# A four-layer graph network on one core: edges on 125 partitions, self-counts in the count matrix, norm sums on VectorE

## The chip, the core and the metric

The kernel runs on one core of a Trainium2 chip. The core has five engines, each with its own in-order queue: PE (TensorE, matrix products; its weight loads are listed as PEld), DVE (VectorE), ACT (ScalarE), POOL (GpSimd) and SP (SyncE, which here only issues DMAs). DMAs are issued from SP, ACT and POOL and are carried by the core's 16 DMA engines. The metric is device time in microseconds (us) of one execution; lower is better.

## What is computed

A graph of N = 6250 nodes with D = 64 features and E = 206250 edges, sorted by destination, goes through four layers, and after each of them `x = layernorm(x + layer(x))`:

```
layer 0: Z[n] = sum over edges e into n of relu([x[src[e]], edge_attr[e]] @ M_W.T + M_b);  relu([x, Z] @ U_W.T + U_b)
layer 1: two GCN convolutions, 64 -> 32 -> 64, relu between
layer 2: attention with 4 heads over the edges into each node (softmax by destination), + bias + x
layer 3: two GCN convolutions, 64 -> 64 -> 64, batch norm over the nodes and leaky relu after each
gcn(h, W, b)[n] = sum over e into n of h'[src[e]] * d[src[e]] * d[n]  +  h'[n] * d[n]^2  +  b,
                  h' = h @ W,  d = rsqrt(in-degree + 1)
```

The second term of `gcn` is each node's own contribution (its self-loop).

## The kernel before

**Tiling.** Nodes stand in NB = 49 blocks of L = 128, the last with NL = 106. Edges stand in supertiles of L partitions with J = 30 successive edges each: LJ = 3840 edges, so S = 54 supertiles, of which the last has only LP = 91 partitions (`of(s)` gives the number). The order of all instructions is the order of the program text (`manual_schedule`); each engine's queue is in that order.

**Start (lines 96 to 424, 707 to 748).** SP loads `x`, then all destinations `dst_i` (L126, L128, L129: rows of 30 integers, 120 bytes each), some weights, then three copies of the edge list on 125 partitions with 1650 edges each (`ef` L350, `en` L352, `sf` L354), two tiles of edge features `xe` (L643), the sources `src_i` (L126, L128, L129 again), `hl_d`, and some thirty small weights and rows. ACT writes the table `tab_d` of transformed nodes to DRAM. VectorE makes from the destinations the window positions `dst_w` and the digits `dst_h`, `dst_l`; from `ef`, `en`, `sf` a check and `hl`; from the last weights (L730 to L739) some products; from `src_i` the row numbers `src_sb` (L133 to L135); and adds up `x_part` (L745). Only then does it come to the loop of layer 0.

**Layer 0 (lines 749 to 782).** Iteration s issues the fetches of supertile s (SP: `xe`, 960 KB; POOL: 30 indirect gathers of one row of `tab_d` per partition into `g`, L433, three buffers) and computes supertile s - 1 (`messages`): PE turns `xe` (L662) and multiplies it (L676), VectorE adds to `g` (L680) and copies `we` (L682), ACT takes relu (L687), VectorE makes one-hot rows of the destinations (L474), and 60 PE instructions (L484) add the messages up in a window, which VectorE adds to `acc` (L487). At five places in each supertile `fill()` puts in one step of a side job. The first side job, `degrees`, is S steps of counting (VectorE: L524, L527; PE: L518) and one that closes it; it gets the first n_count = S // 5 + 1 = 11 iterations. The second, `adjacency`, takes the other S - n_count = 43: 25 count matrices of 2 x 128 destinations by all sources, in 8 steps each (VectorE: one-hots L591, L594 and a check L610; PE: L603; ACT: L605 to fp8), which ACT sends to `adj_d` (L613, 1568 KB each). Side operands such as `iota_c` stand in PSUM. The last supertile goes through `last_messages`.

**Layers 1 and 3** are each two calls of `aggregate`: 13 groups of up to four node blocks. In a group PE multiplies the features (split into three bf16 parts) with the count matrices that SP loads back from `adj_d` (L862, L871); ACT takes the sums out (L843); PE adds the node's own features through the identity (L846) and folds the parts (L848); then comes `post`. In layer 3 `post` is that of `sums_for`: it scales and shifts, and adds up h and h^2 over all nodes for the batch norm with two PE products by a matrix of ones per group (L1194, L1195) into two PSUM banks.

**Layer 2 (lines 1015 to 1094)** gathers 54 x 30 rows of `tab2_d` by `src_sb` (POOL), writes them out by edge (`rows_d`), reads them back as runs by node, and works on these.

The loops of `general`, `general_attention` and `message_sums`, at the end, run only when a check finds data that the fast path can't take; they don't run with these inputs.

Of the kernel before, what the change touches and what calls it, by code (L numbers as in the profile page):

```python
# [39 lines left out]
LF = 125  # L41
# [14 lines left out]
def tile_gnn_resnorm(ctx: ExitStack, tc, a, out, J):  # L56
# [7 lines left out]
    LJ = L * J  # L64
    S = -(-E // LJ)
    LP = (E - (S - 1) * LJ) // J
    EP = E // LF
# [5 lines left out]
    assert E == LF * EP and E == (S - 1) * LJ + LP * J and L <= 2 * LP and EP <= J * L // 2  # L73
# [48 lines left out]

    def load_edges(o, v, s0, s1=S):

        full = min(s1, S - 1)
        nc.sync.dma_start(o[:, s0:full, :], v[s0 * LJ:full * LJ].rearrange("(s p j) -> p s j", p=L, j=J))  # L126
        if s1 == S:
            nc.sync.dma_start(o[0:LP, S - 1, :], v[(S - 1) * LJ:E].rearrange("(p j) -> p j", j=J))  # L128
            nc.sync.dma_start(o[LP:L, S - 1, :], v[E - (L - LP) * J:E].rearrange("(p j) -> p j", j=J))  # L129

# [24 lines left out]
    dst_w = keep.tile([L, S, J], F32, name="dst_w")  # L155
    src_sb = keep.tile([L, S, J], I32, name="src_sb")
# [115 lines left out]
    src_1 = pk.tile([L, S1, J], I32, name="src_1")  # L272
    dst_h = pk.tile([L, S, J], BF16, name="dst_h")
    dst_l = pk.tile([L, S, J], BF16, name="dst_l")
    ohd = st0.enter_context(tc.tile_pool(name="ohd", bufs=2))
# [5 lines left out]
    src_i = pp.tile([L, S, J], I32, name="src_i")  # L281
    lo_i = pp.tile([L, S, J], I32, name="lo_i")
    dig_f = pp.tile([L, EP], F32, name="dig")
    dig = dig_f[:, 0:S * J].rearrange("p (s j) -> p s j", j=J)

    def early(pool, shape, name, like, dtype):

        t = pool.tile(like, dtype, name=name)
        n = 1
        for k in shape[1:]:  # L290
            n *= k
        f = "p j w -> p (j w)"
        return (t.rearrange(f)[0:shape[0], 0:n * 4 // (2 if dtype == BF16 else 4)]).bitcast(I32)

    dst_i = early(ohd, [L, S, J], "oA", [L, J, L], BF16).rearrange("p (s j) -> p s j", j=J)
    d_f = dst.rearrange("(p i) -> p i", p=LF)
    ef = early(ohp, [LF, EP], "oh", [L, J // 2, W], F32)
    en = early(ohp, [LF, EP], "oh", [L, J // 2, W], F32)
    sf = early(ohd, [LF, EP], "oA", [L, J, L], BF16)
    nc.scalar.dma_start(src_i[:, 0:S1], src[0:S1 * LJ].rearrange("(s p j) -> p s j", p=L, j=J))  # L300
    load_edges(dst_i, dst, 0)
# [34 lines left out]
    def ends_in(b):  # L336

        return min(S, -(-(a_block * (b + 1) + SLACK + R) // LJ)) - 1
# [14 lines left out]
    nc.sync.dma_start(en[0:LF - 1, EP - 1:EP], d_f[1:LF, 0:1])  # L353
    nc.sync.dma_start(sf, src.rearrange("(p i) -> p i", p=LF))  # L354
# [3 lines left out]
    in_psum = ps_c.tile([128, W + 1 + 2 * NB], F32, name="pc")  # L358
# [6 lines left out]
    for i in range(2):  # L365
        nc.vector.tensor_copy(iota_2[i * R:(i + 1) * R, i * NB:(i + 1) * NB], iota[i * R:(i + 1) * R, 0:NB])

# [25 lines left out]
    ends = small.tile([L, 2, S], F32, name="ends")  # L393
# [3 lines left out]
    for i, op in enumerate((OP.min, OP.max)):  # L397
        pe = ps_t.tile([S, L], F32, name="pt")
        nc.tensor.transpose(pe, ends[:, i, :], ident[:L, :L])
        nc.vector.tensor_reduce(end2[:, i:i + 1], pe, AX.X, op)  # L400
# [11 lines left out]
    pb = ps_t.tile([L, S], F32, name="pt")  # L412
    nc.tensor.matmul(pb, ones[0:1, :L], win_f[:, 0, :], start=True, stop=True)
    base_b = small.tile([L, S], F32, name="base_b")
    nc.vector.tensor_copy(base_b, pb)
    nc.vector.tensor_sub(dst_w, dst_w, base_b[:, :, None].to_broadcast([L, S, J]))

    d_e = dig_f[0:LF]
    nc.vector.tensor_sub(d_e, ef, en)
    nc.vector.tensor_reduce(bad4[0:LF, 0:1], d_e, AX.X, OP.max)  # L420
    nc.vector.tensor_copy(d_e, sf)
    hl = pp.tile([LF, EP, 2], BF16, name="hl")
    digits(hl[:, :, 0], hl[:, :, 1], sf, en, d_e)
    nc.vector.tensor_scalar_add(hl[:, :, 0], hl[:, :, 0], 1.0)

    def of(s):

        return LP if isinstance(s, int) and s == S - 1 else L

# [13 lines left out]
    def at(t, s):  # L443

        return t[0:of(s), s] if isinstance(s, int) else t[:, ds(s, 1)].rearrange("p o j -> p (o j)")

    def edges_of(t_d, s):

        n = of(s) * J
        v = t_d[s * LJ:s * LJ + n, :] if isinstance(s, int) else t_d[ds(s * LJ, n), :]  # L450
        return v.rearrange("(p j) c -> p j c", j=J)

    def all_supertiles(body):

        with tc.For_i(0, S - 1, 1) as s:
            body(s)
        body(S - 1)

    def row_of_edges(pool, v, s):

        n = of(s)
        n_i = pool.tile([L, J], I32, name="n_i")
        nc.sync.dma_start(n_i[0:n], edges_of(v.rearrange("(e o) -> e o", o=1), s).rearrange("p j o -> p (j o)"))
        lo_i = pool.tile([L, J], I32, name="lo_i")
        n_f = pool.tile([L, J], F32, name="n_f")
        row_of(n_i[0:n], n_i[0:n], lo_i[0:n], n_f[0:n])
        return n_i[0:n]
# [3 lines left out]
    def one_hot(ohp, rel, j0, places):  # L471
        n = rel.shape[0]
        oh = ohp.tile([L, JH, W], F32, name="oh")
        nc.vector.tensor_tensor(oh[0:n], places[0:n, None, :].to_broadcast([n, JH, W]),  # L474
                                rel[:, j0:j0 + JH, None].to_broadcast([n, JH, W]), op=OP.is_equal)
        return oh

    def add_window(ohp, vals, c, rel, base, places=iota):
        n = rel.shape[0]
        pa = sums_in[-1].tile([c, W], F32, name="pa")  # L480
        for j0 in range(0, J, JH):
            oh = one_hot(ohp, rel, j0, places)
            for j in range(JH):
                nc.tensor.matmul(pa, vals[0:n, j0 + j, 0:c], oh[0:n, j, :], start=(j0 + j == 0),  # L484
                                 stop=(j0 + j == J - 1))
        span = acc[0:c, ds(base, W)]
        nc.vector.tensor_add(span, span, pa)  # L487
# [7 lines left out]
    def windows(s, v, window):  # L495

        rel = small.tile([L, J], F32, name="rel")[0:of(s)]
# [13 lines left out]
    def degrees(ohd, todo):  # L511
# [3 lines left out]
        def products(i, o_h, o_l):  # L515
            n = of(todo[i])
            for j in range(J):
                nc.tensor.matmul(count, o_h[0:n, j, :], o_l[0:n, j, :], start=(i + j == 0),  # L518
# [3 lines left out]
        for i, s in enumerate(todo):  # L522
            o_h = ohd.tile([L, J, L], BF16, name="oA")
            nc.vector.tensor_tensor(o_h, iota_c[:L, None, 0:L].to_broadcast([L, J, L]),  # L524
                                    dst_h[:, s, :, None].to_broadcast([L, J, L]), op=OP.is_equal)
            o_l = ohd.tile([L, J, NB], BF16, name="oB")
            nc.vector.tensor_tensor(o_l, iota_c[:L, None, 0:NB].to_broadcast([L, J, NB]),  # L527
                                    dst_l[:, s, :, None].to_broadcast([L, J, NB]), op=OP.is_equal)
# [37 lines left out]
    def adjacency(adp, ohd):  # L566
# [41 lines left out]
        def check(c, q0, adj):  # L608
# [3 lines left out]
            if q0 + QS == L:  # L612
                nc.scalar.dma_start(adj_d[c].bitcast(I8), adj.rearrange("p l a q -> p (l a q)").bitcast(I8))  # L613
# [26 lines left out]
    with st0:  # L640
        def fetch_xe(s):
            xe = l0.tile([L, J, D], F32, name="xe")
            nc.sync.dma_start(xe[0:of(s)], edges_of(xe_in, s))  # L643
            return xe

        def fetch_g(s):
            g = gp.tile([L, J, D], F32, name="g")
            gather(g, D, tab_d, at(src_1 if s < S1 else src_sb, s))
# [5 lines left out]
        def messages(pool, s, xe, g, first_time, fill=lambda: None, then=None):  # L654

            m = of(s)
            we = pool.tile([L, J, H], F32, name="we")

            def turned(k):
                pt = ps_t.tile([128, 3, L], F32, name="pt")  # L660
                for i in range(3):
                    nc.tensor.transpose(  # L662
                        pt[:, i, 0:m], xe[0:m, 6 * k + 2 * i:6 * k + 2 * i + 2, :].rearrange("p a c -> p (a c)"),
                        ident[:m, :m])
                xT = pool.tile([128, 3, L], F32, name="xT", bufs=3)
                nc.scalar.copy(xT[:, :, 0:m], pt[:, :, 0:m])  # L666
                return xT[:, :, 0:m]

            xTs = [turned(0)]
            for k in range(J // 6):  # L670
# [3 lines left out]
                pm = ps_m.tile([L, 3, 2 * CW], F32, name="pm")  # L674
                for i in range(3):
                    nc.tensor.matmul(pm[0:m, i, :], xT[:, i, :], w_bd_f, start=True, stop=True)  # L676
                fill()
                pv = pm[0:m].rearrange("p i (a c) -> p (i a) c", a=2)
                js = slice(6 * k, 6 * k + 6)
                nc.vector.tensor_add(g[0:m, js, :], g[0:m, js, :], pv[:, :, 0:D])  # L680
                if first_time:
                    nc.vector.tensor_copy(we[0:m, js, :], pv[:, :, D:CW])  # L682
                if then:
                    nc.scalar.activation(g[0:m, js, :], g[0:m, js, :], AF.Relu)
                    then(js)
            if not then:
                nc.scalar.activation(g[0:m], g[0:m], AF.Relu)  # L687
            if first_time:
                nc.sync.dma_start(edges_of(we_d, s), we[0:m])
            return g  # L690

        def last_messages(s, xe, g):

            rel, n = at(dst_w, s), of(s)
# [3 lines left out]
            def add(js):  # L698
                for j in range(js.start, js.stop):
                    nc.tensor.matmul(pa, g[0:n, j, :], ohs[j // JH][0:n, j % JH, :], start=(j == 0), stop=(j == J - 1))  # L700
# [8 lines left out]
        load_edges(src_i, src, S1)  # L709
        nc.sync.dma_start(hl_d[0:E, :].rearrange("(p i) k -> p i k", p=LF), hl)  # L710
# [40 lines left out]
        with ExitStack() as st1:  # L751
            adp = st1.enter_context(tc.tile_pool(name="adp", bufs=2))
# [602 lines left out]
```

## Time and profile before

| | |
|---|---|
| device time, median of 3 runs | 5386.54 us (5385.71 to 5386.94) |
| profiled execution, its own time | 7038.8 us |
| its span | 7036.9 us |
| busy share of the span | PE 31%, DVE 40%, ACT 11%, POOL 47% |
| mean granted PE clock | 0.625 of full speed |
| first layer-0 gather | at 22.9 us |
| first step of the loop's side job on VectorE (L524) | at 152.6 us |
| layer 0 ends (L705), layer 1 begins | at 3818 us |
| first gather of layer 2 | at 4131 us |
| last gather of layer 2 | at 6434 us |

The profiled execution took 1652 us more than the runs without a profile. A profile's row of waits names the engine that waited, its instruction and what released it; "issue" and "remote" are releases that it can't name. In a timeline row the first two numbers are start and duration, and the bracket holds the idle time of the engine just before, with its releaser.

### The profile page before, as it was taken

The page shows a single profiled execution, that of the slowest core. Times are in us where ns is not written, and L with a number is a line of the kernel's source. Part 1 is how long each engine was busy: PE and PEld are TensorE (multiplying, and loading weights), DVE is VectorE, ACT ScalarE, POOL GpSimd, SP SyncE. Part 2 cuts the span into 40 slices and gives each one's busy share as a digit, 9 for nine tenths or more (in the row PEclk, how much of TensorE's full clock was granted, in tenths as well). Part 3 has the DMA queues.
Part 4 walks back from the last instruction along what each step waited for, and adds up shares of the span by engine and source line. Part 5 has one row for each costly group of instructions (what it writes and reads, how often), then busy time and mean ns, then how long its engine had stood idle before and what let it go on. Part 6 is the DMA issues. An engine that isn't in the chain of part 4 may idle for free.

```text
span 7036.9 us, 47855 instructions
## 1 busy us (share of the span) xinstructions
PE 2174.8 (31%) x18313; PEld 1664.4 (24%) x18314; DVE 2823.7 (40%) x2744; ACT 795.3 (11%) x1615; POOL 3317.3 (47%) x3350
## 2 busy tenths in 40 slices
PE   1443333333333323333336940000000000001998
PEld 1332323232323323232335520000000000001554
DVE  3554545454544545454455213233232332332012
ACT  0000011111111211111122100000000000000011
POOL 5334353444434343444431037777777777774000
PEclk5665566666666666666666975555555555555998
DMA  3011111111111111111112733233333332333442
GB/s 79 24 31 27 31 39 40 47 42 45 43 47 42 49 39 50 37 51 37 52 40 84 287 108 102 88 100 103 91 107 93 100 100 88 100 100 115 186 156 93
DMA packets 200187, 543.55 MB, mean 77 GB/s; under 512 B 110070, under 2 KB 112386, under 8 KB 178316
## 3 DMA queue, kind: packets, MB, share of 16 engines
q0 software_dynamic: 112336, 219.94, 11.9%
q1 hardware_dynamic: 67188, 273.57, 10.5%
q10 hardware_dynamic: 20424, 46.89, 1.8%
q8 instruction: 146, 2.39, 0.1%
q14 instruction: 93, 0.76, 0.0%
HBM read 434.86 MB, written 105.30 MB: 77 GB/s over the span
## 4 chain that ended last, share of the span: by engine, by line
PE 21%; POOL 19%; another core or an unknown queue 18%; issue 16%; DVE 8%; ACT 4%; DMA 2%; DVEq 0%; ACTq 0%; POOLq 0%; SPq 0%
POOL g L433 18%; PE pA L871 8%; PE pa L484 6%; DVE oB L594 2%; ACT adj L605 2%; DVE oA L591 2%; PE pA L603 1%; PE pm L676 1%; DVE most_a L610 1%; DMA rows<-rows_d,first 1%; ACT g L687 1%; PE pt L662 1%; DVE g L680 1%; PE pm L848 1%
## 5 line engine op out<-in xcount | busy, mean ns | idle before, releaser
L433 POOL DMA_INDIRECT g<-tab_d,src_sb x3120 | 3085.1, 989 | 2936.2 <-issue 2499.8
L603 PE MATMUL pA<-oB,oA 128*128 128x98 bf16 x3200 | 301.6, 240 | 1465.1 <-ACT adj L605 956.7
L591 DVE TENSOR_TENSOR oA<-pc,hlT 128x2048 bf16<-128x2048 f32 x200 | 456.7, 2283 | 598.7 <-remote 302.9
L177 PE MATMUL pt<-ident,acc 128*128 128x128 f32 (+1 forms) x50 | 14.0, 373 | 2155.4 <-issue 1359.3
L603 PEld LDWEIGHTS <-oA 128*128 128x128 bf16 x3200 | 237.3, 117 | 1529.9 <-issue 1500.5
L484 PE MATMUL pa<-oh,g 128*64 128x128 f32 x3180 | 477.0, 326 | 363.9 <-ACT g L687 355.2
L484 PEld LDWEIGHTS pa<-oh,g 128*64 128x64 f32 x3180 | 465.7, 171 | 371.8 <-ACT g L687 371.8
L605 ACT CAST adj<-pA 128x392 fp8e4<-128x392 f32 x800 | 360.1, 488 | 1555.7 <-remote 1178.1
L177 PEld LDWEIGHTS pt<-ident,acc 128*128 128x128 f32 (+1 forms) x50 | 6.2, 173 | 2164.2 <-issue 2150.4
L871 PE MATMUL pA<-adj,three 128*32 128x512 fp8e4 (+3 forms) x4949 | 478.1, 368 | 1.8 <-ACT three L243 1.8
L1025 DVE TENSOR_TENSOR g<-g,we 128x120 f32<-128x120 f32 (+1 forms) x54 | 15.4, 285 | 1051.7 <-DMA g<-tab_d,src_sb 928.1
L676 PE MATMUL pm<-w_bd,xT 128*128 128x136 f32 (+1 forms) x1620 | 343.6, 362 | 56.1 <-issue 39.9
L594 DVE TENSOR_TENSOR oB<-pc,hlT 128x1568 bf16<-128x1568 f32 x200 | 355.7, 1779 | 0.0
L610 DVE TENSOR_REDUCE most_a<-adj 128x1 f32<-128x1568 int8 x200 | 354.8, 1774 | 0.0
L1055 DVE TENSOR_REDUCE hb<-rows 128x64 f32<-128x4096 f32 x46 | 336.6, 7318 | 0.0
L524 DVE TENSOR_TENSOR oA<-pc,dst_h 128x3840 bf16<-128x3840 f32 x54 | 224.2, 4153 | 271.3 <-remote 271.3
L680 DVE TENSOR_TENSOR g<-g,pm 128x384 f32<-128x384 f32 (+1 forms) x270 | 147.3, 545 | 446.2 <-remote 389.3
L676 PEld LDWEIGHTS pm<-w_bd,xT 128*128 128x128 f32 (+1 forms) x1620 | 298.7, 259 | 79.9 <-issue 50.0
L871 PEld LDWEIGHTS <-three 128*32 128x32 bf16 (+1 forms) x5096 | 215.0, 97 | 233.9 <-issue 19.9
L666 ACT COPY xT<-pt 128x384 f32<-128x384 f32 (+1 forms) x270 | 124.0, 479 | 1165.6 <-PE pt L662 601.3
L1043 ACT COPY same<-pA 128x256 f32<-128x256 f32 x49 | 18.3, 372 | 1992.6 <-issue 1851.5
L1052 DVE TENSOR_TENSOR rows<-rows,pA 128x4096 f32<-128x4096 f32 x49 | 216.7, 4422 | 38.5 <-issue 32.2
(253 smaller groups left out, 2579.3 us busy)
## 6 DMA issues: line engine op xcount, KB each, us to landing
adj<-adj_d SPq DMA_DIRECT2D x95, 1568.0 KB
rows_d<-g SPq DMA_DIRECT2D x53, 1020.0 KB
xe<-in_edge_attr_dram SPq DMA_DIRECT2D x53, 960.0 KB
g<-tab_d,src_sb POOLq DMA_INDIRECT x3120
adj_d<-adj ACTq DMA_DIRECT2D x25, 1568.0 KB
we_d<-we SPq DMA_DIRECT2D x53, 60.0 KB
we<-we_d ACTq DMA_DIRECT2D x53, 60.0 KB
g<-tab_d,src POOLq DMA_INDIRECT x120
```

The lines of the kernel that those rows point to most:

```text
L433: nc.gpsimd.indirect_dma_start(out=g[0:n, j, 0:c], out_offset=None, in_=table[:, :], in_offset=bass.IndirectOffsetOnAxis(ap=idx[:, j:j + 1 ...
L484: nc.tensor.matmul(pa, vals[0:n, j0 + j, 0:c], oh[0:n, j, :], start=(j0 + j == 0), stop=(j0 + j == J - 1))
L524: nc.vector.tensor_tensor(o_h, iota_c[:L, None, 0:L].to_broadcast([L, J, L]), dst_h[:, s, :, None].to_broadcast([L, J, L]), op=OP.is_equal)
L591: nc.vector.tensor_tensor(o_h, iota_c[:, None, 1:L + 1].to_broadcast([128, QS, L]), hlT[:, 0, q0:q0 + QS, None].to_broadcast([128, QS, L]) ...
L594: nc.vector.tensor_tensor(o_l, iota_2[:, None, :].to_broadcast([128, QS, 2 * NB]), hlT[:, 1, q0:q0 + QS, None].to_broadcast([128, QS, 2 * ...
L603: nc.tensor.matmul(pA[:, q].rearrange("p a l -> p (a l)"), o_h[:, q1 + q, :], o_l[:, q1 + q, :], start=True, stop=True)
L605: nc.scalar.copy(adj[:, :, :, q0 + q1:q0 + q1 + 4], pA.rearrange("p q a l -> p l a q"), saturate=False)
L610: nc.vector.tensor_reduce(most_a[:, (c * L + q0) // QS:(c * L + q0) // QS + 1], adj[:, :, :, q0:q0 + QS].bitcast(I8), AX.XYZ, OP.max)
L676: nc.tensor.matmul(pm[0:m, i, :], xT[:, i, :], w_bd_f, start=True, stop=True)
L680: nc.vector.tensor_add(g[0:m, js, :], g[0:m, js, :], pv[:, :, 0:D])
L871: nc.tensor.matmul(pa[ps, 0:nk, 0:w], t[:, b, :], adj[:, 0:nk, b, 0:w], start=start, stop=stop)
L1055: nc.vector.tensor_reduce(hb[:, b, :], rows[:, :, 0:D].rearrange("p r c -> p c r"), AX.X, OP.add)
```

## The change

Edges are now tiled on LE = 125 partitions in layer 0, in its counting and in the loops at the end. 125 x 30 = 3750 edges divide E exactly: S = 55 full supertiles. The 125 partitions hold for the tiles and for the DMAs that fill them (`dst_i`, `src_i`, `xe`, `we_d`) and for the rows of each gather; n_count becomes 55 // 5 + 1 = 12, and 43 iterations remain for `adjacency`. Layer 2 keeps 128 partitions (S2 = 54): its row numbers `src2` are made anew from the sources in layer 1 (`sources`, three DMAs and L133 to L135 once more), while `src_sb` lives only in layer 0. The pool `ohd` is opened after `prep` is closed, and the early integer tiles have places of their own instead of places inside `ohd` and `ohp`.

After a count matrix's last check VectorE adds the identity (kept in PSUM beside `iota_c`) to the 128 x 128 part that holds the block's own nodes, two per matrix, 49 in all; the matrix is then sent to `adj_d` from SP instead of ACT. L846 goes. In layer 3 VectorE adds h and h^2 into `both`, two additions per group, and one PE product with the ones follows after the last group.

```diff
-    LJ = L * J
-    S = -(-E // LJ)
-    LP = (E - (S - 1) * LJ) // J
-    EP = E // LF
+    LJ = LE * J
+    S = E // LJ
+    LJ2 = L * J
+    S2 = -(-E // LJ2)
+    LP2 = (E - (S2 - 1) * LJ2) // J
+    EP = E // LE
...
-    load_edges(dst_i, dst, 0)
+    nc.sync.dma_start(dst_i, dst.rearrange(by_edge, p=LE, j=J))
...
-    in_psum = ps_c.tile([128, W + 1 + 2 * NB], F32, name="pc")
+    in_psum = ps_c.tile([128, W + 1 + 2 * NB + L], F32, name="pc")
...
+    ident_c = in_psum[:, W + 1 + 2 * NB:]
+    nc.vector.tensor_copy(ident_c, ident)
...
             if q0 + QS == L:
-                nc.scalar.dma_start(adj_d[c].bitcast(I8), adj.rearrange("p l a q -> p (l a q)").bitcast(I8))
+
+                for a in range(min(2, NB - 2 * c)):
+                    v = adj[:, 2 * c + a, a, :]
+                    nc.vector.tensor_tensor(v, v, ident_c, op=OP.add, saturate=False)
+                nc.sync.dma_start(adj_d[c].bitcast(I8), adj.rearrange("p l a q -> p (l a q)").bitcast(I8))
...
-            xe = l0.tile([L, J, D], F32, name="xe")
-            nc.sync.dma_start(xe[0:of(s)], edges_of(xe_in, s))
+            xe = l0.tile([LE, J, D], F32, name="xe")
+            nc.sync.dma_start(xe, edges_of(xe_in, s))
...
-        load_edges(src_i, src, S1)
+        nc.sync.dma_start(src_i[:, S1:S], src[S1 * LJ:E].rearrange(by_edge, p=LE, j=J))
...
+            ohd = st1.enter_context(tc.tile_pool(name="ohd", bufs=2))
             counting = degrees(ohd, list(range(S)))
...
-            nc.tensor.matmul(pm[:, 0:nb, :], ident, v[:, bs, :], start=True, stop=False)
             for r in range(nb):
-                nc.tensor.matmul(pm[:, r, :], sa[:, r * L:(r + 1) * L], stack[0:m, 0:c], start=False, stop=(r == nb - 1))
+                nc.tensor.matmul(pm[:, r, :], sa[:, r * L:(r + 1) * L], stack[0:m, 0:c], start=True, stop=True)
...
+    def sources(k):
+
+        if k != 4:
+            return
+        n = S2 * J
+        n2, lo2, f2 = (acc[:, i * n:(i + 1) * n].rearrange("p (s j) -> p s j", j=J) for i in range(3))
+        n2, lo2 = n2.bitcast(I32), lo2.bitcast(I32)
+        nc.sync.dma_start(n2[:, 0:S2 - 1, :], src[0:(S2 - 1) * LJ2].rearrange("(s p j) -> p s j", p=L, j=J))
+        nc.sync.dma_start(n2[0:LP2, S2 - 1, :], src[(S2 - 1) * LJ2:E].rearrange("(p j) -> p j", j=J))
+        nc.sync.dma_start(n2[LP2:L, S2 - 1, :], src[E - (L - LP2) * J:E].rearrange("(p j) -> p j", j=J))
+        row_of(src2, n2, lo2, f2)
+        nc.vector.tensor_add(x, x, bc(g1_b2, D))
...
+            if first_one:
+                nc.scalar.activation(both[:, 1], h, AF.Square)
+                nc.vector.tensor_copy(both[:, 0], h)
+                return
             sq = ag.tile([L, 4, D], F32, name="sq")[:, 0:nb, :]
             nc.scalar.activation(sq, h, AF.Square)
+            n = NL if bs.stop == NB else L
+            nc.vector.tensor_add(both[0:n, 0, 0:nb, :], both[0:n, 0, 0:nb, :], h[0:n])
             yield
-            lhsT = ones_l if bs.stop == NB else ones
-            stop = bs.stop == NB
-            nc.tensor.matmul(ps_1[:, 0:nb, :], lhsT, h, start=first_one, stop=stop)
-            nc.tensor.matmul(ps_2[:, 0:nb, :], lhsT, sq, start=first_one, stop=stop)
-            yield
+            nc.vector.tensor_add(both[0:n, 1, 0:nb, :], both[0:n, 1, 0:nb, :], sq[0:n])
             if bs.stop == NB:
-                for i, p in enumerate((ps_1, ps_2)):
-                    nc.vector.tensor_reduce(stat[:, i, :], p.rearrange("p b c -> p c b"), AX.X, OP.add)
+                nc.vector.tensor_reduce(stat, both.rearrange("p i b c -> p i c b"), AX.X, OP.add)
+                pm = ps_m.tile([L, 2, D], F32, name="pm")
+                nc.tensor.matmul(pm, ones, stat, start=True, stop=True)
+                nc.vector.tensor_scalar_mul(stat, pm, 1.0 / N)
...
```

## Prediction

> **What bounds the kernel now.** I first read the busy time by stretch, cut where the stages change. Columns: stretch, its length, then busy us (and instructions) of PE, weight loads, VectorE, ACT, POOL, then granted PE clock, DMA share, GB/s.
>
> ```profile
> 153.00:3818.00 3665.00, 1307.64 (x10544) 1167.25 (x10544) 1848.96 (x1518) 579.87 (x1130) 1495.04 (x1580) 0.63 0.13 40
> 3818.00:4130.00 312.00, 298.68 (x4372) 169.00 (x4371) 95.03 (x265) 61.70 (x185) 0.00 (x0) 0.95 0.61 239
> 4130.00:6437.00 2307.00, 20.73 (x66) 13.41 (x66) 727.28 (x646) 74.51 (x148) 1719.40 (x1667) 0.50 0.31 94
> 6437.00:7037.00 600.00, 519.26 (x3176) 289.54 (x3176) 111.30 (x231) 70.38 (x136) 2.86 (x3) 0.91 0.39 150
> ```
>
> Layer 1 (second row) and layer 3 (fourth) are PE's; layer 2 (third) is POOL's gathers; in layer 0 no engine is much over half busy. So the waits come next, for 153 to 3818 us:
>
> ```profile
> POOL g L433 <- issue: 2038.9, 1506, 80.3
> PEld L603 <- issue: 1500.5, 411, 27.7
> ...
> DVE g L680 <- remote: 389.3, 31, 17.5
> DVE acc L487 <- PE pa L484: 374.4, 53, 7.8
> ```
>
> Most of layer 0's waits have no releaser on record, in pieces up to 28 us. The one that the program explains is VectorE's for the 60 products of each window: 374 us. VectorE's busy 1849, these 374 and the 153 us before make 2376 us, not 3818: 1442 us of unexplained holds, where the runs without a profile are 1652 us shorter. Layer 2's gathers start 1.25 us apart where nothing holds them (0.95 + 0.30), so its 1669 would take 2086 us, not 2307: another 221. I therefore take it that the profile itself slows these two stages. Then 2376 + 312 + 2086 + 600 = 5374, against the median of 5386.5. So in the timed runs **VectorE's queue with its wait for L484 paces layer 0**: 39 us a supertile in the second side job (from 1000 to 3600 us, 38 supertiles: busy 34.0 each, less 2 us in which successive instructions overlap, plus 7.1 of that wait). POOL has 31.1 gathers x 1.25 = 38.9 there: nearly a tie.
>
> **What starts the loop.** Timeline of the start; the last row is the 91st gather, the first that needs a used buffer:
>
> ```profile
> 38.04 25.10 SPq L128 DMA_DIRECT2D src_i<-in_src_dram  x1
> ...
> 45.02 1.88 DVE L419 TENSOR_TENSOR dig<-oh 125x1650 f32<-125x1650 int32 x1 [12.12 <-DMA oh<-in_dst_dram]
> ...
> 85.98 0.23 DVE L730 TENSOR_TENSOR wa<-wn,r_L_gnn_attn_key 128x64 f32<-128x64 f32 x1 [24.12 <-DMA r_L_gnn_attn_key<-in_L_gnn_attn_key_dram]
> ...
> 223.81 0.95 POOL L433 DMA_INDIRECT g<-tab_d,src  x1 [80.26 <-issue]
> ```
>
> VectorE waits for a small row that SP issued behind everything else; SP itself stood 25 us in the issue of `src_i`. Counting begins after that, and POOL stands until the first messages are done. A later start thus moves all of layer 0, whichever engine paces it.
>
> **The change, part by part.**
>
> *Start: +50 us.* The trace has 125-partition loads already: `ef` and `en` (1.61 MB, issued from 23.3) land at 45.0, `sf` 10 us later: 80 GB/s. DMA share while they load:
>
> ```profile
> 24.00:28.00 4.00, 0.41 (x1) 0.12 (x1) 4.00 (x4) 0.00 (x0) 3.39 (x3) 0.50 0.30 74
> 36.00:56.00 20.00, 0.26 (x3) 0.02 (x1) 4.75 (x4) 0.59 (x1) 15.42 (x16) 0.63 1.09 196
> 56.00:72.00 16.00, 0.00 (x0) 0.00 (x0) 5.82 (x11) 0.00 (x0) 12.65 (x12) 0.50 0.46 110
> ```
>
> Share 0.30, gathers included, while only 125-partition loads run; it goes over 1 once the 128-partition `xe` and `src_i` come, and falls to 0.46 for a tail. The Trainium skill ("DMA: Bandwidth & Descriptors", section on why a DMA increments its semaphore by 16) says that a DMA is split over the largest number up to 16 that divides the slowest dimensions of both sides, and from SP always over the lowest-numbered engines. That is 16 for 128 partitions and 5 for 125: 5/16 = 0.31 fits the row, and the tail fits five engines that have `ef`, `en`, `sf` to finish first. By this rule the change moves `dst_i`, `src_i` and both first `xe` onto the same five engines, ahead of what VectorE waits for. Per engine: `dst_i` 6875/5 = 1375 rows of 120 bytes instead of 424, `src_i` 1275 instead of 392: 1834 more. A row costs at most 27 ns (`dst_i`: 11.7 us from issue to use, 424 rows, beside the table's writes); I take 20: 37 us. `xe`: 2 x (188 - 60) KB at 161 KB per 10 us: 16 us. Together 53, and I take **50**, since SP's issue of the small rows, not the rings, ends last now. By the byte count alone (2% fewer partitions) it would be 0. Bounds: 0, if the small rows don't queue behind these; 66, at 27 ns. Later `xe` loads take some 12 us, under a supertile's 39, and `ohd` over `prep`'s space waits for the `hl_d` write, which SP issues ahead of the small rows.
>
> *One more supertile: +20 us.* VectorE: one counting step (L524 + L527, 5.7 from start to start), five times L680 + L682 (0.64 apart), two L474 (4.2), L487 (0.28), the wait of 7.1: 20.4. The closing step of the counting takes the new twelfth iteration nearly alone, so no other VectorE work comes with it. POOL's 30 more gathers (37.5 us) lie beside it: from the 91st gather POOL needs 51 x 37.5 + 50 x 1.25 = 1975 us and some 40 for the work behind its last gather, VectorE ten counting supertiles of 42 (seen between two L487, without the hold) and 43 of 39, so 2097: some 80 us of slack. If POOL paces, 37.5 takes the place of 20 and of the next item. Gathers with 91 partitions stand in the trace at 0.95 + 0.30, like those with 128, so 125 save nothing.
>
> *49 additions of the identity: +13 us* at 0.275 (L578, 128x128 with a PSUM operand), in VectorE's pacing queue; 0 if it has slack. SP now waits for them before it issues `adj_d`; behind that stand `we_d`, which waits for the same supertile's VectorE anyway, and the next `xe`, used a supertile later. ACT loses 25 issues of 0.33 us, beside VectorE: 0.
>
> *Layer 1: -5.5, layer 3: -30 us.* Weight loads in a layer-3 group:
>
> ```profile
> 6545.23 0.41 PEld L846 LDWEIGHTS pm<-tab,ident 128*128 128x128 f32 x2
> 6545.66 1.08 PEld L848 LDWEIGHTS pm<-stack,sa 128*128 128x128 f32 x8
> ...
> 6549.09 0.41 PEld L1194 LDWEIGHTS pa<-hb,ones 128*128 128x128 f32 x2
> 6549.52 0.41 PEld L1195 LDWEIGHTS pa<-sq,ones 128*128 128x128 f32 x2
> 6549.95 0.96 PEld L871 LDWEIGHTS <-three 128*128 128x128 bf16 x5
> ```
>
> From start to start L846 costs PE 0.43 and the two sums 0.86, with L871 queued behind. 1.29 x 24 full groups = 31, and 0.5 for the short ones. Layer 1's L846 (half the width) costs 0.22 from start to start: 24 times and two short ones, 5.5. Against it stands the end of each norm: VectorE's two additions, a longer reduction and a PE product in a row instead of two reductions, about 0.65, twice. -35.7 in all; no wait of PE for `adj` is on record, though layer 1 loads 3.1 MB per 9.3 us and might give a few us back. The busy times (14.4 + 14.5 + 14.4 and 10.7) would say -54, but they overlap. VectorE's 48 additions of 0.42 us fill idle time (111 busy of 600).
>
> *`sources`:* its loads go to SP after the first three `adj` loads, whose first buffer is free only when group 0 is done; the next `adj` isn't held. L133 to L135 (3.7 us of VectorE) lie under 9.3 us of PE per group. 0, at worst 4, and 10 if the loads collide. Layer 2 is unchanged.
>
> **Sum:** 50 + 20.4 + 13 - 35.7 = +48. The profiled execution's own 7039 would move by nearer 100, as there a supertile takes 68 us; I apply +48 to the median: **5434**.
>
> **Rivals.**
> - *No shift at the start* (12%): the wait for the row is only SP's issue, and the loads overlap. 20 + 13 - 36 = -2: 5384. For it: hardly 10 us between the rings' tail and the row. Against it: SP's 25 us in one issue.
> - *ACT's queue, faster* (8%): sending `adj_d` holds ACT, which makes the relu that the window's products wait for. Two rows of waits, 5.2 and 4.7 us, name that DMA. At 5 us for each of 25: -125, so 5309; it decides from (48 + 11)/25 = 2.4 us each. Against it: 0.33 us per issue, and the other waits there name PE or VectorE.
> - *Gathers of 125 rows are slower* (5%): spread over fewer engines, 1.4 instead of 1.25 us apiece, 1650 x 0.15 = 248, less POOL's 80 of slack: about 5600. Against it: the 91-row gathers.
> - *POOL paces* (15%): 50 + 37.5 - 36: 5438, the forecast's own side.
>
> **Numbers.** The forecast, with a start shift of 30 to 66, has 60%; 0.2% (11 us) is what a measurement can tell from no change. Slower: the forecast, POOL's case, the slow gathers: 0.78. Same: most of the first rival, 0.12. Faster: the ACT case and a start without shift with hidden additions (-15): 0.10. Range 5383 to 5467: from the unshifted start to 66 us of shift with POOL pacing and a smaller PE gain.
>
> **What would show it.** VectorE's wait before L730 ending near 135 us; DMA share about 0.3 for most of the first 120 us; 55 supertiles, unchanged gather spacing; layer-3 groups 17.05 us apart instead of 18.33. It is wrong if L730 starts before 100 us, or if ACT's waits beside `adj_d` vanish with a shorter layer 0.

## The result and the profile after

The changed kernel takes **5633.88 us** (5632.94 to 5634.22) against 5386.12 (5384.82 to 5386.94): ratio 1.046, 95% interval 1.0442 to 1.0478. The forecast was 5434 (5383 to 5467). On three of the chips used further down the kernel before itself takes 6978 to 7037 us in all of its runs, and the profile that the forecast read is as long (7038.8); the comparison here and every number not marked otherwise is from where it takes about 5386.

A second profile of the kernel before, taken where it takes 5388, stands beside that of the changed kernel (times of the same events; VectorE lines by their number in the kernel before):

| event | before, us | after, us |
|---|---|---|
| first gather of layer 0 | 22.2 | 34.2 |
| first small row used (L730) | 85.4 | 107.6 |
| first window closed (first L487) | 170.3 | 193.2 |
| layer 0 ends (L705) | 2348.8 | 2624.2 |
| first gather of layer 2 | 2657.3 | 2932.1 |
| last gather of layer 2 | 4789.1 | 5064.3 |
| span | 5386.4 | 5632.5 |

Layer 0 ends 275 us later; all behind it is 29 us shorter. Between the first closed window and the end of layer 0 lie 252 of the 275 us, so the place is the loop, not the start. One stretch inside it, first before, then after (columns as in the forecast's first view: PE, weight loads, VectorE, ACT, POOL, clock, DMA share, GB/s):

```profile
1000.00:2000.00 1000.00, 563.49 (x4447) 498.40 (x4446) 821.94 (x700) 297.65 (x608) 713.71 (x757) 0.71 0.26 73
```

```profile
1000.00:2000.00 1000.00, 505.05 (x3938) 446.81 (x3938) 745.34 (x653) 261.05 (x535) 797.47 (x665) 0.68 0.23 66
```

Every engine does less, except POOL: its 665 fetches need more time than 757 did, 1.20 us each instead of 0.94. With the 0.30 us between two of them, 665 x 1.50 fills the 1000 us: POOL never stops. The groups of the changed kernel name it; the first row is layer 2 and the start, the second the rest of layer 0 (busy us, mean ns):

```profile
L415 POOL DMA_INDIRECT g<-tab_d,src x1740 | 1684.0, 968 | 937.5 <-issue 521.1
L415 POOL DMA_INDIRECT g<-tab_d,src_sb x1530 | 1849.8, 1209 | 466.4 <-issue 450.6
```

The same line, table and bytes per row, but the second group fetches 125 rows a time and costs 1209 ns, while layer 2's 128 rows take 0.94 us. VectorE's longest waits in layer 0 (first before, from 200 to 2310 us, then after, from 200 to 2600; the last supertile is left out of both):

```profile
DVE acc L487 <- PE pa L484: 356.7, 51, 7.8
DVE hlT L586 <- PE pt L583: 11.6, 25, 0.5
```

```profile
DVE acc L466 <- PE pa L463: 370.5, 53, 7.8
DVE g L661 <- DMA g<-tab_d,src_sb: 144.8, 40, 8.7
DVE used L558 <- DMA slots<-hl_d,first: 46.0, 1, 46.0
```

Its wait for the products is as before; new are 191 us of waits for data that POOL gathers (second and third row), and no such row stood there before. In the chain that ended last, POOL has 49% of the changed kernel's span (35% before).

### The profile page after: what moved, and what is told of

It is laid out like the page before. It is cut to its first block, busy times and chain, and to the rows that moved or that the text cites. A ratio compares the mean times of both kernels' runs of the same rounds, so it can differ in the third digit from the quotient of the medians.

```text
span 5632.5 us, 48009 instructions
## 1 busy us (share of the span) xinstructions
PE 2091.8 (37%) x18244; PEld 1595.5 (28%) x18245; DVE 2865.9 (51%) x2859; ACT 783.5 (14%) x1621; POOL 3634.3 (65%) x3380
## 4 chain that ended last, share of the span: by engine, by line
POOL 49%; issue 16%; PE 15%; DMA 14%; DVE 4%; ACT 1%; SPq 0%; DVEq 0%; POOLq 0%; ACTq 0%
POOL g L415 48%; PE pA L851 10%; DMA rows<-rows_d,first 9%; DMA g<-tab_d,src 3%; DMA g<-tab_d,src_sb 2%; PE pa L463 1%; PE pm L828 1%; PE pm L183 1%; DVE oB L572 1%; POOL slots L421 1%; DVE oA L569 1%; PE pm L1053 0%; DVE oA L502 0%; DVE most_a L588 0%; DVE g L661 0%
## 5 line engine op out<-in xcount | busy, mean ns | idle before, releaser
L415 POOL DMA_INDIRECT g<-tab_d,src x1740 | 1684.0, 968 | 937.5 <-issue 521.1
L415 POOL DMA_INDIRECT g<-tab_d,src_sb x1530 | 1849.8, 1209 | 466.4 <-issue 450.6
L463 PE MATMUL pa<-oh,g 125*64 125x128 f32 x3240 | 481.5, 324 | 553.3 <-ACT g L668 544.5
L463 PEld LDWEIGHTS pa<-oh,g 125*64 125x64 f32 x3240 | 470.1, 170 | 563.3 <-ACT g L668 563.3
L657 PE MATMUL pm<-w_bd,xT 128*125 128x136 f32 x1650 | 330.1, 350 | 45.9 <-DVE we L663 26.1
L657 PEld LDWEIGHTS pm<-w_bd,xT 128*125 128x125 f32 x1650 | 279.2, 242 | 78.6 <-DVE we L663 43.3
L661 DVE TENSOR_TENSOR g<-g,pm 125x384 f32<-125x384 f32 x275 | 148.8, 541 | 190.4 <-DMA g<-tab_d,src_sb 167.5
L1034 DVE TENSOR_TENSOR pA<-rows,pa 128x256 f32<-128x256 f32 x49 | 21.0, 429 | 417.7 <-DMA rows<-rows_d,first 417.7
## 6 DMA issues: line engine op xcount, KB each, us to landing
xe<-in_edge_attr_dram SPq DMA_DIRECT2D x55, 937.5 KB
```

The source lines that it names most:

```text
L415: nc.gpsimd.indirect_dma_start(out=g[0:n, j, 0:c], out_offset=None, in_=table[:, :], in_offset=bass.IndirectOffsetOnAxis(ap=idx[:, j:j + 1 ...
L463: nc.tensor.matmul(pa, vals[:, j0 + j, 0:c], oh[:, j, :], start=(j0 + j == 0), stop=(j0 + j == J - 1))
L657: nc.tensor.matmul(pm[:, i, :], xT[:, i, :], w_bd_f, start=True, stop=True)
L661: nc.vector.tensor_add(g[:, js, :], g[:, js, :], pv[:, :, 0:D])
```

## The experiments

**1. What a gather costs by its rows, measured alone.** A kernel with nothing but 30 gathers of 256-byte rows at each of thirteen row counts, then loads of `edge_attr` on different numbers of partitions; the computation is left out.

> This kernel leaves out the whole computation. It issues 30 indirect gathers of 256-byte rows at each of 128, 127, 126, 125, 124, 120, 112, 104, 100, 96, 91, 64 and 32 rows, and then plain loads of different numbers of partitions. Theory 1 (a gather's time on POOL hangs on how its row count divides, not on its size): 125 rows take about 1.21 us as in the changed kernel, 128, 112, 96 and 64 rows about 0.94, 127 at least 1.21; in plain loads 125 partitions of xe take about 16/5 of the time of 128. Theory 2 (the rows are innocent, the gathers of the changed kernel are slowed by what runs beside them): 125 rows take 0.94 us here, like 128. Theory 3 (time goes with the number of rows): 64 rows take half of 128, and 125 a little less than 128.

Groups of this kernel (30 gathers each; the mean ns is the second number behind the bar; `g_bch` is 127 rows, `g_bce` 124, `g_bcf` 125, `g_baa` 100, `g_bcg` 126, `g_bci` 128, `g_jg` 96):

```profile
L33 POOL DMA_INDIRECT g_bch<-in_x_dram,idx x30 | 76.2, 2541 | 9.2 <-issue 9.2
L33 POOL DMA_INDIRECT g_bce<-in_x_dram,idx x30 | 38.5, 1282 | 9.1 <-issue 9.1
L33 POOL DMA_INDIRECT g_bcf<-in_x_dram,idx x30 | 35.7, 1191 | 9.1 <-issue 9.1
L33 POOL DMA_INDIRECT g_baa<-in_x_dram,idx x30 | 29.7, 991 | 9.1 <-issue 9.1
...
L33 POOL DMA_INDIRECT g_bcg<-in_x_dram,idx x30 | 29.4, 978 | 9.1 <-issue 9.1
...
L33 POOL DMA_INDIRECT g_jg<-in_x_dram,idx x30 | 27.4, 912 | 9.1 <-issue 9.1
```

128 rows took 944 ns (median). 127 rows cost 2.7 times as much as 126; 64 rows took 901, so it isn't the number of rows, and 125 was dear with nothing beside it, so theories 2 and 3 fall. Divide the rows by the largest divisor up to 16, the rule that the forecast took from the Trainium skill ("DMA: Bandwidth & Descriptors", section on why a DMA increments its semaphore by 16; it states it for DMAs issued from GpSimd too, with an exception for some direct copies): 127 over 1, 124 over 4 (31 rows), 125 over 5 (25), 100 over 10, 126 over 14 (9), 128 over 16 (8), 96 over 16 (6). From 31 to 127 rows on the busiest engine the cost grows by 1259 ns, 13.1 ns a row; 0.87 us + 13 ns per such row gives all thirteen counts to within 37 ns. The trace doesn't number the DMA engines, so their count is the rule's; measured is that the cost follows it. The 91-row gathers that I had read in the forecast are 13 x 7, so they say nothing of 125.

The loads show it as well. VectorE's copy behind each (127, 126, 125, then 124 partitions, 7680 bytes each):

```profile
595.86 0.15 DVE L41 COPY w<-w 127x1 f32<-127x1 f32 x1 [39.62 <-DMA w<-in_edge_attr_dram]
601.23 0.15 DVE L41 COPY w<-w 126x1 f32<-126x1 f32 x1 [5.21 <-DMA w<-in_edge_attr_dram]
610.91 0.15 DVE L41 COPY w<-w 125x1 f32<-125x1 f32 x1 [9.54 <-DMA w<-in_edge_attr_dram]
626.03 0.15 DVE L41 COPY w<-w 124x1 f32<-124x1 f32 x1 [14.97 <-DMA w<-in_edge_attr_dram]
```

39.6, 5.2, 9.5 and 15.0 us. 125 against 126 is 1.8 times, not the 16/5 (to 128) that I had expected. Loads of `dst` follow, in rows of 120 bytes like those of `dst_i`, on 127 and 126 partitions:

```profile
720.52 0.15 DVE L46 CAST w<-t_bch 127x1 f32<-127x1 int32 x1 [60.70 <-DMA t_bch<-in_dst_dram]
728.28 0.15 DVE L46 CAST w<-t_bcg 126x1 f32<-126x1 int32 x1 [7.60 <-DMA t_bcg<-in_dst_dram]
```

By the same rule the busiest engine has 49 x 127 = 6223 rows in the first and 49 x 126 / 14 = 441 in the second: 9.2 ns a row, where the forecast took 20.

**2. The kernel before once more**, for a profile where it takes 5388 us.

> The kernel before, once more, for a profile that the profiler does not lengthen. Expected: a span near 5385 us, layer 0 over at about 2342 (5386 less the 3008 that the changed kernel needs behind layer 0 and the 36 that layers 1 and 3 saved), gathers 1.25 us apart (0.95 + 0.30). If VectorE paced layer 0, POOL's gathers wait for buffers for some 250 us in all (1620 x 1.25 = 2025 of issue, 50 row loads at 1.25); if POOL paced it, they run without a gap, and layer 0 is over near 2150.

The span was 5386.4 and layer 0 over at 2348.8. POOL's gathers stood still for less than I had put: 1580 of them between 170.9 and 2278.1, at 1.25, leave 132 us. So VectorE's queue paces layer 0, with POOL close behind, at 41.3 us a supertile (170.3 to 2316.7 us, 52 windows).

**3. Gathers of 128 rows in the changed kernel.**

```diff
-    src_sb = pk.tile([LE, S, J], I32, name="src_sb")
-    src_1 = pk.tile([LE, S1, J], I32, name="src_1")
+    src_sb = pk.tile([L, S, J], I32, name="src_sb")
+    src_1 = pk.tile([L, S1, J], I32, name="src_1")
+    nc.vector.memset(src_1[96:L], 0)
+    nc.vector.memset(src_sb[96:L], 0)
...
-            g = gp.tile([LE, J, D], F32, name="g")
+            g = gp.tile([L, J, D], F32, name="g")
...
-            return g
+            return g[0:LE]
```

> The changed kernel, but layer 0's 1650 gathers take 128 rows (rows 125 to 127 fetch row 0 of the table and are not read). Theory 1 (125-row gathers at 1.51 instead of 1.25 us apiece pace layer 0): 1650 x 0.26 = 429 us of POOL work go, VectorE paces layer 0 again, and the time falls to 5386 + 12 to 22 (start) + 20 (one more supertile) - 34 (layers 1 and 3) + 0 to 13 (identity additions), 5384 to 5407. Theory 2 (loads from few DMA engines slow the gathers, whatever their rows): it stays near 5600. Theory 4 (the norm sums and counts hold VectorE): above 5450.

5427.35 us (1.0073 of before, 1.0056 to 1.009), some 20 over the range. **Three rows more per gather, fetched for nothing, take 207 of the 248 us away.** The gathers are at 0.94 us again, and of VectorE's waits for gathered data one of 14.0 us is left. The rest is 39 us: first window at 189.6 (+19.3), from there to the end of layer 0 53.7 more, everything behind it 34.3 less.

**4. The two other parts of the change alone**, on 128 partitions: with both parts; with only the norm sums; with only the self-counts. (The kernel has 54 supertiles, not the 49 that the first expectation names.)

> The kernel before with the two other parts of the change alone: self-counts in the count matrix, and norm sums on VectorE; edges stay on 128 partitions, layer 0 has 49 supertiles and gathers of 128 rows. Theory 1: layers 1 and 3 save their 34 to 36 us, the identity additions cost 0 to 13, so 5350 to 5365, faster than before. Theory 4 (these parts cost time themselves): 5390 or more.

> The kernel before with one part of the change: layer 3's norm sums on VectorE. The two parts together (self_and_sums) gave -21.5 us: layer 0 ended 19.6 us later, all behind it took 41.5 less. Theory A (the 49 identity additions stand in VectorE's pacing queue): they take back all that the self-counts save, so the sums alone are worth the whole gain, 41.5 less 15.5 (L846: 0.22 x 25 + 0.43 x 24), and the time is 5386 - 26 = 5360 (5355 to 5366). Theory B (the 19.6 us have nothing to do with the additions): layer 0 ends later here as well, and the time is 5375 or more.

> The kernel before with one part of the change: the self-counts, 49 additions in layer 0 and adj_d sent from SP, without L846 in layers 1 and 3. Theory A: -15.5 us behind layer 0, +18 to 20 in it, so no gain: 5386 to 5392. Theory C (the additions are hidden, my low end for them): 5386 - 15.5 = 5371.

| | us | ratio (95%) |
|---|---|---|
| both | 5366.48 | 0.9962 (0.9948 to 0.9976) |
| sums alone | 5365.98 | 0.9963 (0.995 to 0.9977) |
| self-counts alone | 5388.29 | 1.0004 (0.9996 to 1.0013) |

The sums are the whole gain: 20.6 us, which is 24 groups of 0.86, the two weight loads that the forecast had counted (with them gone, layer 3's groups are 17.47 us apart instead of 18.33). The self-counts gain nothing: they shorten what comes behind layer 0 by 19.5 us, but from the first closed window to its end layer 0 takes 2196.1 us with them (2191.1 with both parts) against 2178.5 before and 2179.0 with the sums alone. That is 13 to 18 us for 49 additions of 0.286. So theory A holds in kind. Its 19.6, 41.5 and hence 5360 were read at the last window inside the loop; at the end of layer 0, where the stages part, both parts together give +13 (+14 with the start) and -35.7. In both kernels with the self-counts `adj_d` goes from SP; so the shorter layer 0 of the forecast's second rival doesn't show either.

**5. The start.** The loads of `dst_i`, `src_i` and `xe` in two, on 112 and 13 partitions, in the kernel of experiment 3:

```diff
+    def in_two(o, v):
+        for p in (slice(0, 112), slice(112, LE)):
+            nc.sync.dma_start(o[p], v[p])
...
-            nc.sync.dma_start(xe, edges_of(xe_in, s))
+            in_two(xe, edges_of(xe_in, s))
```

> The changed kernel with gathers of 128 rows, and each load of dst_i, src_i and layer 0's xe as two, of 112 and 13 partitions. after_g128 took 5427, its wait for the first small row ended at 104.5 us instead of 85.4, its first window closed 19.4 us later. If the loads from few DMA engines make the start late, the row comes 10 to 19 us sooner (near 90) and the time falls to 5408 to 5418; if the later start has another cause, it stays at 5427; if SP's additional issues count, it is over 5430.

5408.42, some 18 us less (the kernel before was 1.4 us faster beside it than in experiment 3). The small row is used at 86.6 instead of 104.5 us (before: 85.4), the first window closes at 172.4. So the 125-partition loads made nearly all of the later start; 2 us are left.

The same idea used on the three 125-partition loads that the kernel before has already, in the version with both parts (`LF = 110` for 125):

> self_and_sums (5366), but the three copies of the edge list that are checked stand on 110 partitions with 1875 edges each instead of 125 with 1650. If few DMA engines make these loads slow (11 instead of 5 by the rule), VectorE's wait for the first small row ends sooner than at 85 us, by up to 10, and the time falls to 5350 to 5362; VectorE's work on them is 14% longer, some 1 us. If SP's issue of the small rows sets that wait, it stays at 5364 to 5369.

**5354.79 us** (0.994 of before, 0.9925 to 0.9955), 31.8 less than before, where both parts without it gave 21.5: the row is used at 71.7 instead of 85.6. This version beats both kernels; the sums alone with `LF = 110` should give the same and weren't run.

**6. 126 and 127 rows in place**, and `adj_d` sent from ACT instead of SP. For the first two `g`, `src_1` and `src_sb` of experiment 3 get 126 or 127 partitions.

> The changed kernel, layer 0's gathers with 127 rows (rows 125 and 126 fetch row 0 of the table and are not read). Theory 1, in the form that the gathers alone gave it (0.87 us + 13 ns for each row of the busiest DMA engine; engines = largest divisor of the row count up to 16, so 1 for 127): 2.54 + 0.30 us apiece instead of 1.51; 34 + 1650 x 2.84 + 50 x 1.25 + 28 behind the last one + 3008 for the rest = 7820 (7750 to 7900). Theory D (a gather costs by its rows and the price at 125 is peculiar to that number): at most 5650.

> The same with 126 rows (14 engines of 9 rows). Theory 1: 0.98 + 0.30 us apiece, a supertile of gathers 38.4 + 1.25 us, still under the 41.7 of VectorE's queue, so 5427 as with 128 rows (5420 to 5440). Theory D: between 5427 and 5634.

> self_and_sums (5366), but adj_d is sent from ACT again, as before the change. My rival of the forecast (that DMA holds ACT's queue, decisive from 2.4 us for each of the 25): at least 5366 + 60 = 5426. Theory A (the queue is worth nothing, the 18 us in layer 0 are the 49 additions at 0.35 to 0.4 us from start to start): 5362 to 5370. If the wait of SP's queue for the additions is what costs, under 5360.

> The kernel of after_g126 once more, where the kernel before takes its usual 5386 us. Theory 1: 0.98 to 1.00 + 0.30 us apiece, 30 x 1.30 + 1.25 = 40.2 us a supertile for POOL, under VectorE's 41.7, so 5427 as with 128 rows (5420 to 5440). Theory D: between 5427 and 5634. If the kernel before takes about 6990 again, only the gathers' durations are read.

All of these ran where the kernel before took 6978 to 7037 us. The durations can be read (127 rows, columns start and us):

```profile
4800.13 2.54 POOL L417 DMA_INDIRECT g<-tab_d,src_sb  x1 [0.30 <-issue]
4802.98 2.54 POOL L417 DMA_INDIRECT g<-tab_d,src_sb  x1 [0.30 <-issue]
4805.83 2.55 POOL L417 DMA_INDIRECT g<-tab_d,src_sb  x1 [0.31 <-issue]
```

2.54 + 0.30 us apiece; the last of layer 0 at 4805.8, where the sum (34 + 1650 x 2.84 + 50 x 1.25) gives 4782. In its one run the kernel took 8000.12, 100 over the range, as layer 2's gathers take 2302 us there instead of 2132. With 126 rows a gather took 1.00 us, so the price holds in place. But the time, 6817.32 and 6894.19, was below that of the kernel before on the same chips (0.9749 and 0.9802), which no theory had said. Both parts with `adj_d` from ACT took 6960.22 (0.9952, 0.9938 to 0.9965).

**7. On one such chip, side by side:**

> The changed kernel itself, as the partner on the same chip of the next run. Where the kernel before takes 5386 us: 5634. Where it takes about 7000, layer 0 is held by something that is not POOL's gathers; 1650 x 1.51 + 97 = 2590 of gathers then lie under a layer 0 of some 3500, and the time is no more than 1% over that of 126 rows.

> The changed kernel with gathers of 126 rows in layer 0. Theory 1: 1.00 + 0.30 us apiece; where the kernel before takes 5386 us: 5427 (5420 to 5440), 207 us under the changed kernel beside it. Theory D: between 5427 and 5634. Where the kernel before takes about 7000: some 6800 to 6900, within 1% of the changed kernel.

> self_and_sums with adj_d sent from ACT. Rival of the forecast (that DMA holds ACT's queue, decisive from 2.4 us for each of 25): 60 us or more over self_and_sums beside it. Theory A (the queue is worth nothing): within 5 us of it.

> The partner of self_act_again: 5366 where the kernel before takes 5386.

| on this chip | us | ratio (95%) |
|---|---|---|
| before | 7029.96 | |
| the changed kernel (125 rows) | 5811.62 | 0.8269 (0.8255 to 0.8283) |
| the same with 126 rows | 6860.08 | 0.9753 (0.9737 to 0.977) |
| both parts, `adj_d` from SP | 6996.48 | 0.9953 (0.9937 to 0.997) |
| both parts, `adj_d` from ACT | 6994.13 | 0.995 (0.9934 to 0.9967) |

`adj_d`'s queue is worth nothing on this chip: the two intervals overlap. Where the kernel before takes 5386 us, ACT against SP in the same version wasn't run. My expectation of 125 against 126 rows was plainly wrong: here the slow gathers win by 1048 us. Beside each other, 125 rows, then 126:

```profile
1000.00:2000.00 1000.00, 506.33 (x3956) 450.37 (x3957) 749.61 (x658) 267.70 (x539) 797.56 (x665) 0.69 0.24 66
```

```profile
1000.00:2000.00 1000.00, 363.53 (x2755) 327.10 (x2755) 529.83 (x462) 193.53 (x382) 471.49 (x474) 0.63 0.16 46
```

The first row is the changed kernel's from the other chip to within 3%. In the second the compute engines do some 70% of the work, and POOL issues 474 instead of 665, with pauses. The timeline of the 126-row kernel shows where:

```profile
1134.48 1.00 POOL L417 DMA_INDIRECT g<-tab_d,src_sb  x1 [0.30 <-issue]
1135.60 0.56 DVE L663 TENSOR_TENSOR g<-g,pm 125x384 f32<-125x384 f32 x1 [9.80 <-remote]
1135.79 1.00 POOL L417 DMA_INDIRECT g<-tab_d,src_sb  x1 [0.30 <-issue]
...
1140.53 0.87 ACT L585 CAST adj<-pA 128x392 fp8e4<-128x392 f32 x2 [14.93 <-remote]
1141.06 0.87 PE L583 MATMUL pA<-oB,oA 128*128 128x98 bf16 x8 [19.92 <-ACT adj L585]
```

While POOL gathers back to back, VectorE stands 9.8 us, ACT 14.9 and PE 19.9. VectorE goes on just ahead of POOL's last gather, ACT and PE some 4 us after its end. Over 1200 to 1520 us, by slices of 1 us, PE is busy 26% of the time in slices that POOL gathers in and 54% in those where it doesn't; in the kernel before where it takes 5388 us it is busy 53% in slices with gathers, and with 125 rows on this chip 51%. This shows when the engines stand, not why. With 126 rows POOL's longest pause from 1000 to 2400 us is 29.7 us, with 125 rows 0.3 us, and with 127 it is the same from 200 to 2500.

The changed kernel itself points the same way. Its layer 0 takes 2431 us from the first window on this chip as on the other, but its layer 2, which gathers 128 rows, 2303 us from first to last gather instead of 2132: 171 of the 178 us by which it is slower here.

## Why the prediction was wrong

The direction was right, and the other terms were off by at most 31 us; one step was missing 207 us, and it is this sentence of the forecast: **"Gathers with 91 partitions stand in the trace at 0.95 + 0.30, like those with 128, so 125 save nothing."** That 125 save nothing was right; that they cost nothing was not. By the rule the comparison row had 13 engines, 125 has 5. The forecast had that rule in hand and applied it to SP's loads alone. Of its own signs, "unchanged gather spacing" failed: 1.51 us instead of 1.25. Its third rival, given 5%, was what happened. That its 5600 lies near 5634 is in part luck: it put the gather at 1.4 us (it is 1.51) and POOL's slack at 80 us (it is some 200), and the two errors cancel.

- *The gathers.* 1560 of them lie behind the first closed window: 1560 x 0.26 = 406 us more of POOL work. From that window to the end of layer 0, 199 came through (2431.0 us against 2232.2 with 128 rows), so some 207 was slack. The forecast's 80 stood on 43 supertiles at 39 us and ten at 42; 53 at 41.7, as measured with 128 rows, make 2210 instead of 2097, so 113 are added, together 193.
- *"VectorE's queue with its wait for L484 paces layer 0": right*, with POOL a near second (experiment 2). "The profile itself slows these two stages": not so, kernels take as long in runs without a profile (experiments 6 and 7). The conclusion drawn from it, a layer 0 of 2376 us, was near 2349, and layer 2's 2086 below 2132: two misses that offset each other in the sum of 5374.
- *Start, +50 at a bound of 0 to 66:* the row came 19.1 us later with 128-row gathers and 22.2 in the changed kernel, not 50. The mechanism is shown (experiment 5); both terms were mis-sized. By experiment 1 the 1834 rows at 9.2 ns make 17 us instead of 37, and two `xe` at 4.3 us more each (9.5 against 5.2) 9 instead of 16: an estimate of 26, still over the 19 to 22 measured.
- *One more supertile, +20.4:* layer 0 grew by 53.7 from its first window, less 13 to 18 for the additions: 36 to 41, nearly a whole supertile (41.7). The forecast counted VectorE's work alone. The 12th counting iteration, with only the closing step, takes 24.9 us in the kernel of experiment 3, but the next one 50.7: in it VectorE stands 14.0 us for `slots`, whose gathers are queued on POOL behind the next supertile's 30. That is one part of the difference; the others I haven't separated.
- *49 additions, +13:* 13 to 18 (experiment 4).
- *Layers 1 and 3, -35.7:* behind layer 0 everything is shorter by 34.3 us with 128-row gathers, by 35.7 in experiment 4 with both parts and by 29.3 in the changed kernel itself. The groups of layer 3 are 17.03 us apart instead of 18.33, as forecast (17.05). The match to the tenth is chance: with both parts layer 1 gives 1.7 us instead of 5.5, though its groups are 9.10 us apart instead of 9.33 as counted, and layer 3 33.0 instead of 30. What takes the rest back is open.
- *`sources` and `adj_d`'s queue, 0:* nothing of either shows. The second rival (125 us off layer 0 once ACT is free of `adj_d`) is out: in experiment 4 layer 0 grew by 13 to 18 us with `adj_d` from SP, about what 49 additions of 0.286 account for.

Without the gathers the sum of the forecast, +48, would have stood beside a measured +39, but only because start and supertile are off in opposite directions.

## What to carry to other kernels

Before you change the number of partitions of anything that a DMA moves, factor it: 125 is 5 x 25, and a gather of 125 rows costs 1.21 us where 126 and 128 cost 0.98 and 0.94. Where gathers pace a stage, a few padded rows are cheaper: 5427 against 5634 us here, though on the chip of experiment 7 the padded kernel was the slower one, so measure both. Price an operation from a row of the trace only if it agrees in what sets the cost, here the largest divisor up to 16, not in looking similar. And compare profile and median first: when they differ by 30%, ask for the condition in which the profile was taken before explaining its holds.

## What the runs showed of the hardware, unexpected

- The price of an indirect gather on POOL: 0.87 us + 13 ns for each row on the busiest DMA engine, counted by the rule of experiment 1, from 32 to 128 rows (863 to 2541 ns).
- Loads: 937.5 KB on 125 partitions 9.5 us, 945 KB on 126 5.2 us, 952.5 KB on 127 39.6 us.
- Two conditions: about 5386 and about 7030 us for the same kernel before. In the second, engines that wait for each other stand 9.8 to 19.9 us in the stretch shown while POOL gathers 126 rows, and layer 2 with 128 rows takes 171 us longer; with 125 or 127 rows POOL has no pause over 0.3 us in layer 0, and the change is a gain of 17%. Not settled: what puts a chip into one of the two (each was measured at one time only, so chip and time aren't told apart), and whether the number of DMA engines behind each gather (by the rule 14 and 16 against 5 and 1) makes the difference or POOL's pace: between 5 and 14 engines nothing was run. The verdict on the change, 4.6% slower, is that of the first condition.
